# Edge tiles over one fixed range of 16 targets each, and their sums joined by transpositions

## The chip, the cores and the metric

The kernel runs on one core of a Trainium2 chip. The metric is the device time of one execution in microseconds (us), taken as the median of several runs. TensorE (PE) multiplies matrices into PSUM, VectorE (DVE) and ScalarE (ACT) work on rows of up to 128 partitions, GpSimd (POOL) issues gathers by an index list, and SyncE (SP) issues plain transfers. Sixteen DMA engines move the data.

## The reference

A graph layer over 16 batches, 1024 nodes and 256 channels. Only the nonzero entries of `adj` count: there are 9052, about 8.8 for each target v and 19 at most.

```python
pre_u = einsum('bud,dk->buk', h, W1[:d]);  pre_v = einsum('bvd,dk->bvk', h, W1[d:])
hidden = relu(pre_u[:, :, None, :] + pre_v[:, None, :, :] + b1)
S   = sigmoid(einsum('buvk,ko->buvo', hidden, W2)[..., 0] + b2[0])
a_t = einsum('buv,bud->bvd', S * adj, h)
m_t = einsum('uv,bud->bvd', adj, h) * h
z   = beta1 * h + beta2 * (einsum('bvd,de->bve', a_t, Wa) + ba) + beta3 * (einsum('bvd,de->bve', m_t, Wm) + bm)
```

## The kernel before, in words

**Blocks, windows, tiles.** The work goes by 4 groups of 4 batches and 8 blocks of 128 targets: 32 blocks (`order`). A block has 2 windows of 64 targets, and a window 5 tiles of 128 edge slots, so there are 320 tiles. The steps of the main loop (L882) are numbered n by tiles; s is the step within a block (0 to 9).

**Lists.** For each of the 8 blocks of targets `lists` (L242) finds on DVE the sources of each target (up to 24 by `max`), counts them, and gives each target its first slot in its window (`first`, L293 to L310). The 640 slots of a window are 5 tiles of 128. Before the change the window has four quarters of 16 targets: quarter 0 fills from slot 0 upward, quarter 1 from slot 128 on, quarters 2 and 3 fill from their ends downward, so the tiles 0, 1, 3 and 4 are full and the free slots lie in the middle of tile 2. `uidx` holds the source of each slot, and an index beyond the table for an empty one; `val` the entry of `adj`; `onehot` which of 16 targets a slot belongs to. Slot i of a tile lies on partition i.

**One tile.** `fetch` (L515) has POOL issue a gather of up to 128 rows of 8192 bytes from `table[g]`: for the 4 batches of a group the products `pre_u` and the values h of a source. Eight buffers `fetched` take the gathers in turn; a buffer is free again when the sums of its tile are done (`gather_in`, L873), and only then is the gather eight tiles later issued. `expand` (L610, PE) spreads `pre_v` over the slots, `add` (L646, DVE) adds it to the fetched rows, `gate` (L650) takes relu and the product with W2 for 4 batches on DVE (L656), the sigmoid on ACT (L659) and multiplies the one-hot rows by it on ACT (L661). `left_adj` (L619, ACT) has multiplied them by the entry of `adj` (L625).

**Edge sums.** `aggregate` (L664, PE) multiplies the one-hot rows (128 slots by 32 columns: 16 targets, with and without the gate) by the fetched h (128 by 256) for 4 batches, which stand side by side in 4 times 32 columns of PE. That is one pass of 4 multiplications; each shows as two MATMUL in the profile. Before the change a tile holds targets of one or two quarters (`QUARTERS`), so a window takes 1+2+2+2+1 = 8 passes. Two quarters share one PSUM tile `acc` (each its own half); after tile 2 and after tile 4 `half_end` (L678) copies it to `ev` on ACT (L681).

**Turning over.** `turn_over` (L683) transposes `ev` on PE (L691, four transpositions for 32 targets and 256 channels) and copies the result to `LT` on ACT (L694); `times_h` (DVE, L705) multiplies one half by h. It is called twice for a window (q = 0, 1). `block_end` (L710) multiplies `LT` by Wa and Wm (L722), and SP writes the output.

**Other traffic.** SP and ACT also load transposed h for later products, write the tables, and copy h into them (L434, L439, L465); their places are fixed to step numbers. The order on every engine is the order of the code (`manual_schedule`, L492).

## Time and profile before

| What | Value |
|---|---|
| runs of the kernel before | 1075.23 us median; 1073.11 and 1077.70 the others |
| span of the profiled execution | 1080.4 us, 5.2 us above that median |
| busy: PE, DVE, ACT, POOL | 1020.1, 1017.6, 862.6, 459.3 us |
| mean transfer rate | 365 GB/s, 394.56 MB in all |

The profile is of one execution; its groups name a line, an engine, the tiles written and read, the number of instructions, their busy time and mean length, and the idle time ahead of them with what ended it. The view by stages gives for a stretch of the span the busy time of each engine and the mean share of time in which the 16 DMA engines had a packet under way. A share over 1 means that packets of one engine overlap. Beside the views, the trace has a record of each DMA packet: queue, start, length and size.

### The profile page before, as it was taken

What the parts mean: (1) busy time and instruction counts of PE and PEld (TensorE: products, weight loads), DVE (VectorE), ACT (ScalarE), POOL (GpSimd) and SP (SyncE); (2) the same over time, 40 slices, a digit from 0 to 9 for tenths busy, and PEclk for the clock granted to TensorE, in tenths of its full rate; (3) what the DMA queues carried; (4) which work ended last, traced back from release to release, by engine and by line L of the source; (5) the groups of instructions that cost most, each with busy time, mean ns of one, the idle gap of its engine ahead of it and who ended that gap; (6) DMA issues with size and microseconds to landing.
All of it is one profiled execution on the core that took longest, in us unless ns stands there. A gap on an engine that the chain in (4) does not pass through costs nothing.

```text
span 1080.4 us, 24120 instructions
## 1 busy us (share of the span) xinstructions
PE 1020.1 (94%) x7673; PEld 731.3 (68%) x7673; DVE 1017.6 (94%) x3481; ACT 862.6 (80%) x2616; POOL 459.3 (43%) x456
## 2 busy tenths in 40 slices
PE   7777999999999999999999999999999999999996
PEld 6654676776666776677777767777766667666654
DVE  8687999998999999999999999999999999999993
ACT  3246787788888887898888888889889889999983
POOL 2666676555257334553333334333333333333330
PEclk9989999999999999999999999999999999999999
DMA  9999899999999999999999999999999999999991
GB/s 283 327 340 385 313 339 381 362 382 378 403 352 371 408 381 385 379 403 395 404 393 399 412 384 392 408 396 389 381 361 370 369 348 368 365 381 369 365 341 44
DMA packets 147752, 394.56 MB, mean 365 GB/s; under 512 B 18224, under 2 KB 94512, under 8 KB 111408
## 3 DMA queue, kind: packets, MB, share of 16 engines
q0 software_dynamic: 50544, 301.16, 70.9%
q1 hardware_dynamic: 83776, 78.66, 22.9%
q10 hardware_dynamic: 13296, 13.11, 3.5%
q8 instruction: 63, 1.03, 0.4%
q14 instruction: 73, 0.60, 0.1%
HBM read 396.93 MB, written 50.33 MB: 414 GB/s over the span
## 4 chain that ended last, share of the span: by engine, by line
PE 40%; DVE 34%; issue 10%; ACT 8%; DMA 5%; POOL 2%; another core or an unknown queue 0%; POOLq 0%; DVEq 0%; ACTq 0%
DVE fetched L656 16%; DVE fetched L648 12%; PE acc L673 10%; PE misc L722 10%; PE misc L445 9%; PE pc L615 7%; DMA fetched<-table,uidx 3%; PE misc L691 2%; ACT left L661 2%; DVE LT L705 1%; ACT X L489 1%; PE misc L449 1%; DVE low L484 1%; DVE h_blk L737 1%; DMA hT__635<-in_xT_dram 1%
## 5 line engine op out<-in xcount | busy, mean ns | idle before, releaser
L518 POOL DMA_INDIRECT fetched<-table,uidx x320 | 339.4, 1061 | 529.0 <-PE acc L673 389.0
L656 DVE SCALAR_TENSOR_TENSOR fetched<-fetched,w_b 128x256 f32<-128x256 f32 x1280 | 478.0, 419 | 0.0
L648 DVE TENSOR_TENSOR fetched<-fetched,pc 128x1024 f32<-128x1024 f32 x320 | 387.7, 1212 | 29.9 <-PE pc L615 19.4
L661 ACT ACTIVATE left<-left,gt 128x32 f32<-128x32 f32 (+1 forms) x1280 | 299.6, 305 | 10.4
L673 PE MATMUL acc<-fetched,left 128*32 128x256 f32 x4096 | 273.4, 385 | 6.3 <-ACT gt L659 3.7
L615 PE MATMUL pc<-X,mark 128*128 128x512 f32 x640 | 243.7, 462 | 10.9 <-DVE fetched L648 9.3
L673 PEld LDWEIGHTS acc<-fetched,left 128*32 128x32 f32 x4096 | 127.6, 109 | 112.1 <-issue 29.1
L615 PEld LDWEIGHTS pc<-X,mark 128*128 128x128 f32 x640 | 105.4, 189 | 88.9 <-issue 41.6
L659 ACT ACTIVATE gt<-sc,b_b 128x4 f32<-128x4 f32 x320 | 95.9, 300 | 46.7 <-DVE fetched L656 37.5
L722 PE MATMUL misc<-w_m,LT 128*128 128x256 f32 x496 | 117.3, 379 | 0.0
L722 PE MATMUL misc<-w_a,LT 128*128 128x256 f32 x496 | 117.2, 379 | 0.0
L445 PE MATMUL misc<-w_v,hT 128*128 128x256 f32 x448 | 107.6, 383 | 0.0
L722 PEld LDWEIGHTS misc<-w_a,LT 128*128 128x128 f32 x496 | 93.8, 189 | 15.3 <-issue 0.4
L722 PEld LDWEIGHTS misc<-w_m,LT 128*128 128x128 f32 x496 | 93.8, 190 | 15.1
L625 ACT ACTIVATE left<-onehot,val 128x64 f32<-128x64 bf16 (+1 forms) x320 | 102.9, 322 | 0.0
L385 POOL DMA_INDIRECT val<-in_adjT_dram,vidx x80 | 87.2, 1090 | 34.4 <-issue 20.4
L656 DVE DVE_READ_ACCUMULATOR fetched<-fetched,w_b 128x1 f32 x1280 | 100.7, 79 | 0.0
L691 PE MATMUL misc<-ident,ev 128*128 128x128 f32 x512 | 79.5, 278 | 18.5 <-issue 7.0
L445 PEld LDWEIGHTS misc<-w_v,hT 128*128 128x128 f32 x448 | 86.4, 193 | 14.3
L691 PEld LDWEIGHTS misc<-ident,ev 128*128 128x128 f32 x512 | 60.7, 141 | 45.7 <-ACT ev L681 15.2
L482 ACT CAST X<-misc 128x512 fp32r<-128x512 f32 x64 | 37.1, 580 | 55.2 <-PE misc L445 48.0
L445 PE MATMUL misc<-w_u,hT 128*128 128x256 f32 x320 | 76.6, 386 | 4.0 <-issue 3.8
(185 smaller groups left out, 1011.3 us busy)
## 6 DMA issues: line engine op xcount, KB each, us to landing
h_blk<-table SPq DMA_DIRECT2D x62, 256.0 KB
out_dram<-h_blk SPq DMA_DIRECT2D x62, 256.0 KB
hT<-in_xT_dram SPq DMA_DIRECT2D x28, 512.0 KB
table<-in_x_dram ACTq DMA_DIRECT2D x24, 512.0 KB
table<-tab SPq DMA_DIRECT2D x48, 256.0 KB
fetched<-table,uidx POOLq DMA_INDIRECT x320
table<-in_x_dram SPq DMA_DIRECT2D x8, 512.0 KB
table<-fetched SPq DMA_DIRECT2D x8, 512.0 KB
```

Of the source, the lines that this page charges most:

```text
L385: nc.gpsimd.indirect_dma_start(out=val[:, i, j:j + 1], out_offset=None, in_=adj_flat, in_offset=bass.IndirectOffsetOnAxis(ap=vidx[:, i, j: ...
L445: nc.tensor.matmul(p[:, bb * D:(bb + 1) * D], hT[:, 2 * h + bb, i, :], wt[:, i, :], start=(i == 0 and not begun), stop=(i == DC - 1), skip ...
L518: nc.gpsimd.indirect_dma_start(out=fetched[at_slot[n]], out_offset=None, in_=table[g], in_offset=bass.IndirectOffsetOnAxis(ap=uidx[:, vt * ...
L615: nc.tensor.matmul(pcs[n][:, c], marks[n // TW][:, j * P:(j + 1) * P], cuts[k][:, w, c], start=True, stop=True)
L625: nc.scalar.activation(lefts[n][:, :m, 1::GB, :], onehot[:, i, o:o + m, :].unsqueeze(2).to_broadcast([P, m, GB // 2, V]), AF.Copy, scale=v ...
L648: nc.vector.tensor_tensor(t, t, pcs.pop(n), ALU.add)
L656: nc.vector.scalar_tensor_tensor(t[:, b, :], t[:, b, :], 0.0, w2_b, ALU.max, ALU.mult, accum_out=sc[:, b:b + 1])
L659: nc.scalar.activation(gt, sc, AF.Sigmoid, bias=b2_b)
L661: nc.scalar.activation(lefts[n][:, :m, 2 * b, :], lefts[n][:, :m, 1 + b // 2 * GB, :], AF.Copy, scale=gt[:, b:b + 1])
L673: nc.tensor.matmul(accs[h][b * 2 * V:(b + 1) * 2 * V, r, :], left[:, i, 2 * b - b % 2:2 * b - b % 2 + 2].rearrange("p k v -> p (k v)"), f[ ...
L691: nc.tensor.transpose(pt[:, r, :, c, :], ev[:, r, c * P:(c + 1) * P], ident)
L722: nc.tensor.matmul(pz[:, bb * D:(bb + 1) * D], LTs[k][:, 2 * h + bb, i if bb else 1 - i, c, :], wt[:, c, :], start=False, stop=(i == 0 and ...
```

## The change

Each tile of a window now holds targets of one fixed range of 16: the ranges begin at targets 0, 11, 24, 37 and 48 of the window's 64 (`FROM`), so neighbours overlap in 5, 3, 3 and 5 targets. A target's edges go on behind those of the target before it, but the targets from `NEW[j]` on (0, 16, 27, 40, 53) start no earlier than slot 128 j. So every tile fills from its slot 0 upward, and its free slots are its last ones. With these inputs all 9052 edges find a slot in both versions; the windows have 549 to 607 edges, and after the change the emptiest tile holds 84, the fullest 128.

`aggregate` makes one pass for a tile. Two tiles that follow each other share one `acc` (also over a window's or block's end), and `pair_end` copies it to one of four `ev` tiles. `turn_over` turns the five tiles of a window, one half of the channels at each call: five transpositions write into one PSUM tile at their targets' columns, and where ranges overlap, PSUM adds. In the last window (`apart`) each call takes the three tiles that touch its 32 targets, for both halves of the channels. For w = 1 both calls stand at s = 2, one ahead of the step's other work and one behind it (before: s = 0 and s = 2). The lists need one multiplication of 5 columns for `first`, and some DVE instructions less; constants are made by 15 small POOL instructions at the start.

On PE in the middle of the kernel, this is what stands there before the change: one step's sums (L673) of three passes, transpositions of two halves (L691), with the expansion of `pre_v` (L615) between them.

```order
L722 MATMUL misc<-w_m,LT 128x256 x4
L615 MATMUL pc<-X,mark 128x512 x2
L691 MATMUL misc<-ident,ev_10157 128x8x16 x4
L673 MATMUL acc_10231<-fetched_171,left 32x256 x8
L673 MATMUL acc_10231<-fetched_172,left 32x256 x4
L673 MATMUL acc_10305<-fetched_172,left 32x256 x4
L615 MATMUL pc<-X,mark 128x512 x2
L691 MATMUL misc<-ident,ev_10229 128x8x16 x4
L615 MATMUL pc<-X,mark 128x512 x2
L691 MATMUL misc<-ident,ev_10313 128x8x16 x4
```

The corresponding place after the change, where the sums are L632, the transpositions L654, the expansion L580, and the product with Wm L688:

```order
L688 MATMUL misc<-w_m,LT 128x256 x4
L580 MATMUL pc<-X,mark 128x512 x2
L654 MATMUL misc<-ident,ev_9315 128x8x16 x2
L654 MATMUL misc<-ident,ev_9383 128x8x16 x2
L654 MATMUL misc<-ident,ev_9452 128x8x16
L632 MATMUL acc_9506<-fetched_167,left 32x256 x4
L632 MATMUL acc_9506<-fetched_168,left 32x256 x4
L580 MATMUL pc<-X,mark 128x512 x2
L654 MATMUL misc<-ident,ev_9315 128x8x16 x2
L654 MATMUL misc<-ident,ev_9383 128x8x16 x2
L654 MATMUL misc<-ident,ev_9452 128x8x16
L580 MATMUL pc<-X,mark 128x512 x2
```

Two tiles take 8 multiplications in place of 16, and each half of the channels five transpositions, from three `ev`, in place of four for each 32 targets.

On ACT, a window's end before the change: the scaled one-hot rows of the middle tiles have 2 by 16 columns (L661, L625), `ev` is copied twice a window (L681), and `LT` by quarters (L694).

```order
L659 ACTIVATE gt<-sc,b_b 128x4
L661 ACTIVATE left<-left,gt 128x2x16 x4
L625 ACTIVATE left<-onehot,val 128x2x16
L694 COPY LT<-misc 128x2x16x16
L681 COPY ev_11392<-acc_11309 128x512
L659 ACTIVATE gt<-sc,b_b 128x4
L661 ACTIVATE left<-left,gt 128x16 x4
```

And after it (L621 the sigmoid, L623 and L588 the scaled rows, L656 the copy to `LT`, L640 that to `ev`):

```order
L621 ACTIVATE gt<-sc,b_b 128x4
L623 ACTIVATE left<-left,gt 128x16 x4
L588 ACTIVATE left<-onehot,val 128x2x16
L656 COPY LT<-misc 128x8x64 x2
L640 COPY ev_10685<-acc_10670 128x512
L621 ACTIVATE gt<-sc,b_b 128x4
L623 ACTIVATE left<-left,gt 128x16 x4
```

Every tile now has the narrow rows; `ev` is copied every second tile.

The diff, cut to its core:

```diff
--- before.py
+++ after.py
@@ -71,12 +71,12 @@
     E = TW * P
     S = 24
     U = W // 2
-    Q = 4
-    V = W // Q
-    QUARTERS = [[0], [0, 1], [1, 2], [2, 3], [3]]
+    V = 16
+    FROM = [0, 11, 24, 37, 48]
+    NEW = [0] + [v + V for v in FROM[:-1]]
     RC = 5 + S
     BIG = float(N * N)
-    assert D == 256 and DC == 2 and NW == 2 and S % 8 == 0 and TW == Q + 1
+    assert D == 256 and DC == 2 and NW == 2 and S % 8 == 0 and FROM[-1] + V == W and len(FROM) == TW
     const = ctx.enter_context(tc.tile_pool(name="const", bufs=1))
     dram = ctx.enter_context(tc.tile_pool(name="dram", bufs=1, space=bass.MemoryType.DRAM))
@@ -123,59 +123,32 @@
     nc.vector.tensor_scalar(soon, row, float(W), None, ALU.is_lt)
-    MID = TW // 2
     inw = fixed([P, 1], "inw")
     nc.vector.scalar_tensor_tensor(inw, late, -float(W), row, ALU.mult, ALU.add)
...
+    bounds = fixed([P, 2, TW], "bounds")
+    for j in range(TW):
+        nc.gpsimd.memset(bounds[:, 0, j:j + 1], float(NEW[j]))
+        nc.gpsimd.memset(bounds[:, 1, j:j + 1], float(FROM[j]))
+    reached = fixed([P, TW], "reached")
+    nc.vector.tensor_scalar(reached, bounds[:, 0, :], inw, None, ALU.is_le)
+    start_ = fixed([P, TW], "start_")
+    nc.vector.tensor_scalar(start_, upto[:, :TW], float(P), BIG, ALU.mult, ALU.add)
+    nc.vector.tensor_tensor(start_, start_, reached, ALU.mult)
+    nc.vector.tensor_scalar(start_, start_, -BIG, None, ALU.add)
     until = fixed([P, 1], "until")
+    nc.vector.tensor_scalar(bounds[:, 1, :], bounds[:, 1, :], inw, None, ALU.is_le, ALU.add, accum_out=until)
+    nc.vector.tensor_scalar(until, until, float(P), None, ALU.mult)
+    place = fixed([P, TW, V], "place")
+    for j in range(TW):
+        nc.gpsimd.tensor_copy(place[:, j, :], upto[:, FROM[j]:FROM[j] + V])
+    before = fixed([P, P], "before")
+    nc.vector.tensor_scalar(before, upto[:, :P], row, None, ALU.is_gt)
+    nc.vector.tensor_scalar(before[:, W:], before[:, W:], late, None, ALU.mult)
     slot_of = fixed([P, NW, TW], "slot_of")
     for w in range(NW):
         nc.vector.tensor_scalar(slot_of[:, w, :], upto[:, :TW], float(P), row, ALU.mult, ALU.add)
     ident = fixed([P, P], "ident")
     nc.vector.tensor_scalar(ident, upto[:, :P], row, None, ALU.is_equal)
     slot, nth = upto, upto[:, :S]
@@ -195,7 +168,7 @@
     uidx = const.tile([P, NT * NW, TW], I32, name="uidx")
     vidx = const.tile([P, NT * NW, TW], I32, name="vidx")
     val = const.tile([P, NT * NW, TW], FP, name="val")
-    onehot = const.tile([P, NT * NW, 2 * Q, V], mybir.dt.bfloat16, name="onehot")
+    onehot = const.tile([P, NT * NW, TW, V], mybir.dt.bfloat16, name="onehot")
     whose = const.tile([P, NT * NW, E], mybir.dt.uint8, name="whose")
     thr = const.tile([P, NT], FP, name="thr")
     rest = const.tile([P, NT], FP, name="rest")
@@ -283,29 +256,24 @@
         nc.vector.memset(R[:, 3:4], 1.0)
         yield "op"
         nc.vector.tensor_copy(R[:, 4:5], inw)
+        yield "op"
+        ahead_ = lst.tile([P, TW], FP, name="ahead", bufs=4)
+        nc.vector.tensor_scalar(ahead_, reached, R[:, 0:1], None, ALU.mult)
         yield "step"
         pw = aside(vt)
-        for i in range(4):
-            nc.tensor.matmul(pw[:, i:i + 1], sums[:, i].rearrange("p w q v -> p (w q v)"), R[:, 0:1],
-                             start=True, stop=True)
+        nc.tensor.matmul(pw[:, :TW], before, ahead_, start=True, stop=True)
         yield "wait"
         first = R[:, 1:2]
-        from_ = lst.tile([P, 1], FP, name="from", bufs=4)
-        nc.vector.tensor_scalar(from_, pw[:, 1:2], base, low_, ALU.add, ALU.max)
-        yield "op"
-        nc.vector.scalar_tensor_tensor(first, from_, high_, pw[:, 0:1], ALU.min, ALU.add)
-        yield "op"
-        nc.vector.tensor_scalar(from_, pw[:, 2:3], second_, since, ALU.add, ALU.max)
-        yield "op"
-        nc.vector.tensor_tensor(from_, pw[:, 3:4], from_, ALU.max)
+        from_ = lst.tile([P, TW], FP, name="from", bufs=4)
+        nc.vector.tensor_tensor(from_, pw[:, :TW], start_, ALU.add)
+        yield "op"
+        nc.vector.tensor_reduce(first, from_, AX.X, ALU.max)
         yield "op"
         held = lst.tile([P, 1], FP, name="held", bufs=4)
         nc.vector.tensor_scalar(held, first, -1.0, until, ALU.mult, ALU.add)
         yield "op"
         nc.vector.tensor_scalar(held, held, 0.0, R[:, 0:1], ALU.max, ALU.min)
-        yield "op"
-        nc.vector.scalar_tensor_tensor(held, first, from_, held, ALU.is_ge, ALU.mult)
         yield "op"
         nc.vector.tensor_tensor(R[:, 0:1], held, first, ALU.add)
         yield "op"
@@ -369,13 +337,9 @@
         wanted.extend((i, j) for i in range(vt * NW, (vt + 1) * NW) for j in range(TW))
         yield "cut"
         col = L.rearrange("p (w j) r -> p w j r", w=NW)
-        for i in range(2):
-            nc.vector.tensor_tensor(
-                onehot[:, sl].rearrange("p w (q i) v -> p w q i v", i=2)[:, :, :, i, :],
-                place.unsqueeze(1).to_broadcast([P, NW, Q, V]),
-                col[:, :, i:i + Q, 4:5].to_broadcast([P, NW, Q, V]), ALU.is_equal)
-            if i == 0:
-                yield "op"
+        nc.vector.tensor_tensor(
+            onehot[:, sl], place.unsqueeze(1).to_broadcast([P, NW, TW, V]),
+            col[:, :, :, 4:5].to_broadcast([P, NW, TW, V]), ALU.is_equal)
     wanted = []
@@ -619,12 +584,10 @@
     def left_adj(n):
         k, g, vt, w, j = where(n)
         i = vt * NW + w
-        m = len(QUARTERS[j])
-        o = max(2 * j - 1, 0)
-        lefts[n] = wk.tile([P, 2, 2 * GB - 1, V], FP, name="left", bufs=5)
-        nc.scalar.activation(lefts[n][:, :m, 1::GB, :],
-                             onehot[:, i, o:o + m, :].unsqueeze(2).to_broadcast([P, m, GB // 2, V]),
-                             AF.Copy, scale=val[:, i, j:j + 1])
+        lefts[n] = wk.tile([P, 2 * GB - 1, V], FP, name="left", bufs=5)
+        nc.scalar.activation(lefts[n][:, 1::GB, :],
+                             onehot[:, vt * NW + w, j, :].unsqueeze(1).to_broadcast([P, GB // 2, V]),
+                             AF.Copy, scale=val[:, vt * NW + w, j:j + 1])
     running = []
     be1_eye = []
@@ -658,43 +620,47 @@
         gt = wk.tile([P, GB], FP, name="gt")
         nc.scalar.activation(gt, sc, AF.Sigmoid, bias=b2_b)
         for b in range(GB):
-            nc.scalar.activation(lefts[n][:, :m, 2 * b, :], lefts[n][:, :m, 1 + b // 2 * GB, :],
+            nc.scalar.activation(lefts[n][:, 2 * b, :], lefts[n][:, 1 + b // 2 * GB, :],
                                  AF.Copy, scale=gt[:, b:b + 1])
     def aggregate(n):
-        k, g, vt, w, j = where(n)
         left, f = lefts.pop(n), fetched[at_slot[n]]
-        for i, q in enumerate(QUARTERS[j]):
-            h, r = divmod(q, 2)
-            first = j == h * MID and r == 0
-            if first:
-                accs[h] = psa.tile([P, 2, D], FP, name=f"acc{h}")
-            for b in range(GB):
-                nc.tensor.matmul(accs[h][b * 2 * V:(b + 1) * 2 * V, r, :],
-                                 left[:, i, 2 * b - b % 2:2 * b - b % 2 + 2].rearrange("p k v -> p (k v)"), f[:, GD + b * D:GD + (b + 1) * D],
-                                 start=first, stop=(j == q + 1), skip_group_check=True)
-    def half_end(n, q):
-        evs[q] = one.tile([P, 2, D], FP, name=f"ev{q}")
-        nc.scalar.copy(evs[q], accs.pop(q))
+        i, r = divmod(n, 2)
+        if r == 0:
+            accs[i] = psa.tile([P, 2, D], FP, name=f"acc{i % 2}")
+        for b in range(GB):
+            nc.tensor.matmul(accs[i][b * 2 * V:(b + 1) * 2 * V, r, :],
+                             left[:, 2 * b - b % 2:2 * b - b % 2 + 2].rearrange("p k v -> p (k v)"),
+                             f[:, GD + b * D:GD + (b + 1) * D], start=(r == 0), stop=True, skip_group_check=True)
+    def pair_end(i):
+        evs[i] = one.tile([P, 2, D], FP, name=f"ev{i % EVS}")
+        nc.scalar.copy(evs[i], accs.pop(i))
     def turn_over(k, w, q, step):
         if w == 0 and q == 0:
             LTs[k] = one.tile([P, GB, 2, DC, P], FP, name="LT")
         LT = LTs[k]
-        pt = small("pt").rearrange("p (r k c v) -> p r k c v", r=2, c=DC, v=V)
-        ev = evs.pop(q)
-        for i in range(4):
-            r, c = divmod(i, DC)
-            nc.tensor.transpose(pt[:, r, :, c, :], ev[:, r, c * P:(c + 1) * P], ident)
-        v = slice(w * W + q * U, w * W + (q + 1) * U)
-        r = (w * W + q * U) // V
-        nc.scalar.copy(LT.rearrange("p b k c (r v) -> p r (b k c) v", v=V)[:, r:r + 2],
-                       pt.rearrange("p r k c v -> p r (k c) v"))
         apart = k == BS - 1 and w == NW - 1
-        if not apart:
+        n = k * T + w * TW
+        def turn(c, of, v0, v1):
+            pt = small("pt").rearrange("p (k v) -> p k v", v=W)
+            for j in of:
+                i, r = divmod(n + j, 2)
+                nc.tensor.matmul(pt[:, :, FROM[j]:FROM[j] + V], evs[i][:, r, c * P:(c + 1) * P], ident,
+                                 is_transpose=True, start=(j == of[0]), stop=True, skip_group_check=True)
+            nc.scalar.copy(LT[:, :, :, c, w * W + v0:w * W + v1].rearrange("p b k v -> p (b k) v"), pt[:, :, v0:v1])
+        if apart:
+            of = [j for j, v in enumerate(FROM) if v < (q + 1) * U and v + V > q * U]
+            for c in range(DC):
+                turn(c, of, q * U, (q + 1) * U)
+            v = slice(w * W + q * U, w * W + (q + 1) * U)
+        else:
+            turn(q, range(TW), 0, W)
             if not q:
                 return
             v = slice(w * W, (w + 1) * W)
@@ -821,7 +787,9 @@
     def products(n, k, s):
         nonlocal end, parts
         made_rows(n)
-        if (s == 2 and 0 < k < BS) or n == total:
+        if s == 2 and 0 < k < BS:
+            turn_over(k - 1, 1, 0, n)
+        if n == total:
             turn_over(k - 1, 1, 1, n)
         z = 3 if n < ROOM else 4
         if z <= s < z + 4 and 0 < k < BS:
@@ -836,8 +804,8 @@
             turn_over(k, 0, 0, n)
         if s == 7 and k == BS - 1 or s == 8 and n < ROOM:
             turn_over(k, 0, 1, n)
-        if (s == 0 and 0 < k < BS) or n == total - 1:
-            turn_over(k - (s == 0), 1, 0, n)
+        if n == total - 1:
+            turn_over(k, 1, 0, n)
         if n == total - 2:
             end = tail(tails[:2], n)
             next(end)
@@ -875,8 +843,8 @@
         free.append(at_slot.pop(n))
         refill()
         fetch_val(1 + (n % 3 == 0))
-        if (n + 1) % TW in (0, MID + 1):
-            half_end(n, 0 if (n + 1) % TW else 1)
+        if n % 2:
+            pair_end(n // 2)
     done = 0
     for n in range(total + 2):
@@ -904,6 +872,8 @@
         do(n)
         if s == 8 and ROOM <= n < LAST:
             turn_over(k, 0, 0, n)
+        if s == 2 and 0 < k < BS:
+            turn_over(k - 1, 1, 1, n)
         if n >= LAST and n + 2 < total:
             expand(n + 2)
         if n == 1:
```

More of the change, by code (lines that the diff above doesn't have):

```diff
@@ L123 @@
     nc.vector.tensor_scalar(soon, row, float(W), None, ALU.is_lt)
-    MID = TW // 2
     inw = fixed([P, 1], "inw")
     nc.vector.scalar_tensor_tensor(inw, late, -float(W), row, ALU.mult, ALU.add)
-    from_q = fixed([P, NW * Q + 1], "from_q")
-    nc.vector.tensor_scalar(from_q, upto[:, :NW * Q + 1], float(V), row, ALU.mult, ALU.is_le)
-    hv = fixed([P, NW, Q, 1], "hv")
-    nc.vector.tensor_tensor(hv.rearrange("p w q one -> p (w q one)"), from_q[:, :-1], from_q[:, 1:], ALU.subtract)
-    mine = fixed([P, Q], "mine")
@@ L160 @@
-    same = hv.rearrange("p w q one -> p (w q) one").to_broadcast([P, NW * Q, V])
-    nc.vector.memset(sums[:, 1:], 0.0)
-    nc.vector.tensor_scalar(ahead, upto[:, :P].rearrange("p (q v) -> p q v", v=V), row, None, ALU.is_gt)
-    nc.vector.tensor_tensor(ahead, ahead, same, ALU.mult)
-    def of(q, n=1):
-        return hv[:, :, q:q + n, :].to_broadcast([P, NW, n, V])
-    nc.vector.tensor_tensor(sums[:, 0, :, 2:, :], sums[:, 0, :, 2:, :], of(2, 2), ALU.subtract)
-    nc.vector.tensor_copy(sums[:, 1, :, 1:2, :], of(0))
@@ L177 @@
     nc.vector.tensor_scalar(ident, upto[:, :P], row, None, ALU.is_equal)
-    place = upto[:, :W].rearrange("p (q v) -> p q v", v=V)
     slot, nth = upto, upto[:, :S]
@@ L508 @@
     BS = NG * NT
+    EVS = 4
     def where(n):
@@ L650, in gate @@
     def gate(n):
-        m = len(QUARTERS[n % TW])
         t = fetched[at_slot[n]][:, :GD].rearrange("p (b d) -> p b d", b=GB)
```

21 lines of the change are left out of this document (removed).

## The prediction

> **What bounds the kernel now.** I read the page first: busy shares, then the DMA lines.
>
> ```profile
> span 1080.4 us, 24120 instructions
> PE 1020.1 (94%) x7673; PEld 731.3 (68%) x7673; DVE 1017.6 (94%) x3481; ACT 862.6 (80%) x2616; POOL 459.3 (43%) x456
> DMA packets 147752, 394.56 MB, mean 365 GB/s; under 512 B 18224, under 2 KB 94512, under 8 KB 111408
> q0 software_dynamic: 50544, 301.16, 70.9%
> q8 instruction: 63, 1.03, 0.4%
> q14 instruction: 73, 0.60, 0.1%
> ```
>
> PE and DVE are both busy for 94% of the span, so neither alone is plainly the limit, and the gathers (queue q0) take 70.9% of all DMA engine time. Packets of 8 KB and more are 147752 - 111408 = 36344; without those of q8 and q14 (63 + 73) they are 36208, which is 4 groups times the 9052 edges: a row of a gather is one packet, and an empty slot moves none of this size.
>
> Next the view by stages, since shares of the whole span mix different limits.
>
> ```profile
> core 0: us, PE busy (x) PEld busy (x) DVE busy (x) ACT busy (x) POOL busy (x), PEclk, DMA share, GB/s
> 80.00:140.00 60.00, 50.42 (x337) 33.31 (x328) 51.77 (x186) 42.67 (x129) 39.25 (x38) 0.94 0.95 343
> 140.00:200.00 60.00, 56.32 (x438) 40.38 (x437) 58.42 (x216) 45.88 (x139) 38.05 (x39) 1.00 1.01 370
> 200.00:300.00 100.00, 95.94 (x725) 68.89 (x722) 96.92 (x336) 81.18 (x250) 47.93 (x49) 1.00 1.01 378
> 300.00:400.00 100.00, 97.46 (x734) 70.26 (x736) 97.70 (x334) 84.97 (x258) 47.67 (x46) 1.00 1.02 382
> 400.00:500.00 100.00, 96.64 (x730) 69.58 (x723) 98.06 (x330) 82.32 (x252) 49.53 (x48) 1.00 1.03 391
> 500.00:600.00 100.00, 99.70 (x785) 72.13 (x784) 95.75 (x319) 88.38 (x275) 34.84 (x34) 1.00 1.02 399
> 600.00:700.00 100.00, 98.66 (x754) 72.12 (x753) 95.64 (x313) 85.47 (x262) 35.95 (x33) 1.00 1.02 398
> 700.00:800.00 100.00, 99.80 (x775) 72.33 (x774) 96.37 (x315) 87.22 (x268) 34.67 (x33) 1.00 1.01 385
> 800.00:900.00 100.00, 96.47 (x764) 66.94 (x767) 99.28 (x330) 90.62 (x283) 36.48 (x36) 1.00 0.97 365
> 900.00:1000.00 100.00, 98.12 (x778) 70.12 (x771) 100.00 (x334) 90.05 (x279) 36.02 (x36) 1.00 0.97 368
> 1000.00:1050.00 50.00, 47.02 (x387) 31.38 (x386) 50.00 (x173) 43.59 (x139) 17.36 (x17) 1.00 0.98 360
> ```
>
> Three resources stand at the edge at once. From 200 to 800 us the DMA share is 1.01 to 1.03, DVE has 2 to 4% left and PE seems full; from 800 on DVE is full and the DMA share is 0.97. The change cuts PE's work, so the question is what stands next behind PE: DVE, with 910 - 888.1 = 21.9 us of idle time between 140 and 1050 us, and the DMA engines.
>
> Whether the DMA engines are full, and how the gathers lie on them, no view says; the records of single packets do. An 8 KB packet of a gather lasts 309 ns in 76% of cases, at any time of the run, and the next of its engine starts 306 ns after it. By these steps the packets of one engine can be followed. On each engine a gather leaves eight packets: 8 KB ones (R) for filled slots and 4-byte ones (z) for empty slots, then one more of 4 bytes that ends it. From 500 to 1040 us 738 such groups of eight could be read without a break:
>
> ```
> RRRRRRRR 535   RRRRzzzz 46   zzzzRRRR 46   zzzzzzzz 41   all others 70
> ```
>
> So an engine always has the same eight slots of a tile, two runs of four slots that stand next to each other, and what an empty slot leaves free is not given to another engine. Slots dealt out one by one would give groups such as RRzzzzzR; the busiest engine would then go from 568 to 596 filled slots, half of what is summed below.
>
> [...]
>
> **The change part by part.** First the gathers, which the diff does not touch, but whose empty slots it moves. Counted from the lists that the two versions make of these inputs, a window of 640 slots has 566 filled on average, 35.4 for each of the 16 engines' 40. Before, the empty ones are in the middle of tile 2. With runs of four at a distance of 32 or of 64 slots the busiest engine has 586 or 576 of the 640 slots filled that it serves over the 80 tiles of a group (mean 566). After, every tile fills from slot 0 and has at least 84 filled, so by either pairing some engines have all 640: 8 rows of every tile in place of 7.2 to 7.3. The price of a row is the 306 ns step (309 as recorded; 338 ns if all of q0's 70.9% is laid on the 2263 rows of an engine). That is 0.67 rows * 306 ns = 0.21 us a tile (0.8 rows for the other pairing, 0.24 us), over 320 tiles 66 us, where the busiest engine ends last.
>
> Where does it? For each stage, in us on the busiest engine (runs 32 apart, the smaller difference): tiles landed, its rows before and after times 306 ns, packets of everything else (recorded time, a sixteenth), and the sums:
>
> ```
> stage       us tiles  rows before/after  other   sum before  sum after
>   80:140    60   17       124    136      18.2       56.2       59.9
>  140:200    60   15       112    120      24.1       58.4       60.8
>  200:300   100   32       240    256      25.8       99.3      104.2
>  300:400   100   30       219    240      33.1      100.1      106.5
>  400:500   100   31       228    248      32.8      102.6      108.7
>  500:600   100   33       240    264      28.3      101.8      109.1
>  600:700   100   34       248    272      27.2      103.1      110.5
>  700:800   100   33       244    264      21.8       96.4      102.6
>  800:900   100   34       252    272      14.4       91.5       97.6
>  900:1000  100   36       266    288      11.7       93.1       99.9
> 1000:1050   50   18       128    144       7.7       46.8       51.7
> ```
>
> Sums up to 3% over the stage say how far recorded times count overlaps twice. Where the sum after is over both the stage and the sum before, the excess is the loss: 0.8 + 4.2 + 6.4 + 6.1 + 7.3 + 7.3 + 2.6 + 1.7 = 36 us. From 700 on the page's share (1.01, 0.97, 0.97) is 5 to 8 points over the mean engine's sum by steps, because 2% of the packets take over 600 ns, up to 2 us. If half of that is real standing time, the three stages from 700 to 1000 lose about 3, 1.5 and 4 us more; I take 9.
>
> The other terms stand beside this, and their rows are:
>
> ```profile
> L673 PE MATMUL acc<-fetched,left 128*32 128x256 f32 x4096 | 273.4, 385 | 6.3 <-ACT gt L659 3.7 <-ACT left L661 2.4
> L691 PE MATMUL misc<-ident,ev 128*128 128x128 f32 x512 | 79.5, 278 | 18.5 <-issue 7.0 <-ACT ev L681 5.0 <-ACT LT L694 3.2
> L661 ACT ACTIVATE left<-left,gt 128x32 f32<-128x32 f32 x768 | 184.0, 310 | 6.2
> L661 ACT ACTIVATE left<-left,gt 128x16 f32<-128x16 f32 x512 | 115.6, 296 | 4.2
> L681 ACT COPY ev<-acc 128x512 f32<-128x512 f32 x128 | 73.1, 571 | 7.0 <-remote 4.2 <-PE acc L673 2.0 <-PE pc L615 0.5
> L373 DVE TENSOR_TENSOR onehot<-upto,L 128x128 bf16<-128x128 f32 x16 | 4.2, 282 | 0.0
> L298 DVE TENSOR_SCALAR from<-misc,second__104,since 128x1 f32<-128x1 f32 x5 | 1.4, 273 | 0.0
> L266 DVE TENSOR_REDUCE cut<-cand 128x1 f32<-128x8 f32 x8 | 1.3, 156 | 0.0
> POOL fetched L518 <- PE acc L673: 389.0, 119, 5.1
> DVE fetched L648 <- PE pc L615: 19.4, 21, 2.0
> DVE fetched L648 <- DMA fetched<-table,uidx: 2.7, 1, 2.7
> ```
>
> *PE.* Passes fall from 8 to 5 a window: 4096 * 3/8 = 1536 MATMUL less at 273.4/4096 = 67 ns, -103 us busy. Transpositions rise from 512 to 63 * 10 + 12 = 642: 130 * 155 ns = +20 us. PE's 1020 us become some 937. The gain counts only where PE ends last. DVE waited for PE's expansion 19.4 us in all, and with the lighter PE that mostly goes; what is late next there is the gather.
>
> *Earlier release.* POOL waited 389 us for the sums that free a buffer. A tile's sums end some 0.5 us sooner (8 MATMUL less). But from a gather's issue to its first packet the records show 4.5 us in the median: the rows wait in the engines' queues, so an earlier issue lengthens that queue. I take 0; if the queues were empty it would be worth up to 0.5 us a tile.
>
> *ACT.* Gates: 768 * 14 ns = -11 us; copies of `ev`: 160 in place of 128, +18 us; the scaling by `adj` has fewer columns in 192 of 320 tiles. Near 0, on an engine with 10% and more left.
>
> *DVE and the start.* A list loses one of two comparisons (L373, 282 ns), and five small instructions (such as L298, 273 ns) become three (such as L266, 156 ns): 0.4 to 1.1 us for each of eight lists, four of them ahead of the first gather. The constants lose as many. I take -2 us, between 0 and -4. POOL's 15 small instructions go ahead of a memory fill that nobody needs for tens of us: 0.
>
> *Waits.* Both transposition calls of w = 1 now stand in step 2, behind the copy of the last `ev` in step 1. ACT's copy to `LT` behind the second call comes after that step's gate, and PE's next use of that PSUM buffer waits for it: one copy (571 ns, as L681) a block at most, 18 us if PE were the limit, 0 while gathers are. I take 0.
>
> Sum: 36 + 9 - 2 = +43 us. The profiled execution lies 5.2 us above the median; the same +43 on both gives 1075.2 + 43 = 1118 us.
>
> **The rivals.** *PE's relief counts.* If the DMA engines have room after all (their share of 1.0 being packets that wait, not work), PE falls by 83 us and DVE ends: its idle 21.9 us between 140 and 1050 go, 1075 - 22 = 1053 us. For it: DVE waits by name for PE (19.4 us), hardly for a gather (2.7 us). Against it: PE's busy time counts ends that overlap; by the steps from one start to the next (at most 216 ns for 256 columns, 236 for 512, 109 for a transposition) its work fills 90 to 92% of the stages from 500 to 800 us, while the DMA share there is over 1. It decides if an engine's rows can run faster than one in 306 ns. *Empty slots are shared out.* If the DMA engines evened out the rows, bytes and sums would stay as they are, the stages from 200 to 700 could not run faster, and only the start and the last stages gain: 1072 us. The groups speak against it. *Full price everywhere.* If the last three stages have no room, the 0.207 us count for all tiles past 80 us: 303 * 0.207 = 63, 1138 us; DVE at 100% there speaks for both being close. That the lists would leave edges to the slow path behind the main loop is excluded: all 9052 find a slot.
>
> **How the numbers follow.** A measurement of this kernel tells 0.5% from no change, 5.4 us. Busiest engine ends last, as summed: 0.75; full price everywhere: 0.14; PE's relief: 0.07; shared out: 0.04. Low end of the forecast's own case: the lower sums if overlaps are taken out of every packet (3 ns each), which leaves +18 to +27 us, so 1093; upper end the full price, 1138. The range 1092 to 1138 leaves out the two faster cases, 0.11, and a little above. Slower 0.89, same 0.04, faster 0.07.
>
> **What would show it.** After the change the stages between 200 and 700 us should hold 28 to 31 tiles in 100 us in place of 30 to 34, DVE should fall to 88 to 92% there with its wait on L648 named for the gathers, PE's sums to 2560 MATMUL and 171 us, and the mean DMA share below 1.0, since eight engines wait for the other eight. Every group of eight packets should be R's followed by z's, none the other way round. I am wrong if the DMA share stays at 1.02 with more tiles in 100 us, or if DVE is over 98% busy throughout.

## The result, and the profile after

The changed kernel takes 1142.18 us (median of 4 runs, 1136.84 to 1146.02), the kernel before 1076.47 us on the same terms (1073.11 to 1080.33). The ratio is 1.061, with an interval of 1.058 to 1.065: slower, by 66 us. The forecast was 1118 us, with a range of 1092 to 1138, so the direction came true, but the time lies above the range and the size was too small by a third.

The page after, the lines that answer to those of before:

```profile
span 1135.0 us, 21191 instructions
PE 982.7 (87%) x6219; PEld 701.8 (62%) x6219; DVE 1014.5 (89%) x3446; ACT 863.9 (76%) x2650; POOL 467.0 (41%) x471
...
DMA packets 147741, 394.37 MB, mean 347 GB/s; under 512 B 18224, under 2 KB 94512, under 8 KB 111408
...
q0 software_dynamic: 50544, 301.16, 68.1%
```

The bytes of the gathers are those of before (301.16 MB), and PE has less to do, but PE, DVE and the mean DMA engine all have a smaller share of a longer span. No engine on the page is busy all the time. The stages (columns as before):

```profile
200.00:300.00 100.00, 90.59 (x569) 63.22 (x568) 94.17 (x326) 79.18 (x244) 47.13 (x47) 0.95 0.98 362
300.00:400.00 100.00, 82.36 (x503) 59.40 (x502) 83.39 (x273) 71.93 (x223) 43.10 (x43) 0.91 0.95 344
400.00:500.00 100.00, 92.64 (x610) 66.89 (x611) 97.86 (x344) 84.39 (x264) 49.17 (x48) 1.00 0.99 370
500.00:600.00 100.00, 78.20 (x491) 56.41 (x490) 79.70 (x262) 67.65 (x209) 27.55 (x27) 0.92 0.95 358
600.00:700.00 100.00, 94.98 (x607) 68.85 (x606) 92.91 (x303) 86.73 (x273) 34.12 (x32) 0.98 0.94 357
700.00:800.00 100.00, 84.18 (x550) 60.40 (x549) 83.69 (x272) 76.30 (x240) 31.60 (x30) 0.93 0.94 347
800.00:900.00 100.00, 90.65 (x588) 64.41 (x588) 96.66 (x319) 85.43 (x269) 34.00 (x33) 0.98 0.95 366
900.00:1000.00 100.00, 92.84 (x629) 65.45 (x628) 99.47 (x329) 90.90 (x279) 38.28 (x35) 1.00 0.93 353
```

Between 200 and 800 us the DMA share was 1.01 to 1.03 and is now 0.94 to 0.99: in the mean, some of the 16 engines stand idle. The stages from 300, 500 and 700 us are much worse than their neighbours, and there every compute engine has a hole: of DVE's additions (L611), one for each tile, 28, 27 and 29 ran in them, against 31, 33 and 33 before, while the stages from 200 and 400 us hold as many as before (30 and 32) and the one from 600 us one less (32). The groups on the additions, the sums and the transpositions, and the waits for transfers and the like, name the new wait and those holes:

```profile
L611 DVE TENSOR_TENSOR fetched<-fetched,pc 128x1024 f32<-128x1024 f32 x320 | 390.0, 1219 | 41.3 <-DMA fetched<-table,uidx 24.6 <-PE pc L580 12.4 <-issue 1.7
L632 PE MATMUL acc<-fetched,left 128*32 128x256 f32 x2560 | 206.4, 396 | 28.0 <-ACT left L623 27.7
L654 PE MATMUL misc<-ident,ev 128*128 128x128 f32 x642 | 97.1, 282 | 58.5 <-ACT tab L425 38.9 <-ACT low L447 12.9 <-ACT ev L640 3.8
```

```profile
ACT tab L425 <- DMA table<-tab: 37.1, 5, 13.8
DVE fetched L611 <- DMA fetched<-table,uidx: 24.6, 27, 4.0
ACT X L453 <- DMA out_dram<-h_blk: 21.3, 2, 14.8
DVE h_blk L703 <- DMA h_blk<-table: 14.1, 2, 9.8
```

DVE waited 2.7 us for gathers before and waits 24.6 now. The last number of a wait is its longest: ACT stood up to 14 us for a table store, and PE and DVE behind it. On the chain of waits these stores show how long they take:

```profile
494.83 30.60 DMA table<-tab
700.40 33.59 DMA table<-tab
```

How a wait becomes a hole can be followed at one place:

```profile
515.90 1.04 ACT L453 CAST X<-low 64x1024 fp32r<-64x1024 f32 x1 [6.53 <-DMA out_dram<-h_blk]
```

ACT had waited 6.5 us for an output store, and PE 4.4 us behind ACT. From 510.2 to 522.6 us no sums ran on PE and no buffer came free, and POOL issued no gather for 11.2 us, up to 523.7 us. In 2 us some 80 rows of gathers ran before; from 522 to 526 us there were 5 in all.

The groups of eight packets, read as in the prediction (from 500 us on, 532 groups), now all have their filled slots ahead but for 21 of them (the last column: 5 zzzzRRRR and 16 mixed ones). The lists of the changed kernel allow no such group, so these 21 are probably misread:

```
RRRRRRRR 418   RRRRzzzz 61   other R..z 32   rest 21
```

### The profile page after: what moved, and what is told of

It reads as the page before. It is cut to its first block, busy times and chain, and to the rows that moved or that the text cites. A ratio compares the mean times of both kernels' runs of the same rounds, so it can differ in the third digit from the quotient of the medians.

```text
span 1135.0 us, 21191 instructions
## 1 busy us (share of the span) xinstructions
PE 982.7 (87%) x6219; PEld 701.8 (62%) x6219; DVE 1014.5 (89%) x3446; ACT 863.9 (76%) x2650; POOL 467.0 (41%) x471
## 3 DMA queue, kind: packets, MB, share of 16 engines
q0 software_dynamic: 50544, 301.16, 68.1%
## 4 chain that ended last, share of the span: by engine, by line
DMA 32%; DVE 29%; PE 21%; ACT 8%; issue 8%; POOL 1%; ACTq 0%; SPq 0%; POOLq 0%; DVEq 0%
DVE fetched L618 13%; DMA table<-tab 12%; DVE fetched L611 10%; DMA fetched<-table,uidx 10%; PE misc L409 6%; PE misc L688 5%; PE acc L632 4%; DMA out_dram<-h_blk 4%; PE pc L580 3%; DMA hT__2450<-in_xT_dram 2%; ACT left L623 2%; PE misc L654 1%; DMA table<-in_x_dram 1%; POOL fetched L483 1%; ACT LT L656 1%
## 5 line engine op out<-in xcount | busy, mean ns | idle before, releaser
L483 POOL DMA_INDIRECT fetched<-table,uidx x320 | 344.1, 1075 | 576.8 <-PE acc L632 390.9
L611 DVE TENSOR_TENSOR fetched<-fetched,pc 128x1024 f32<-128x1024 f32 x320 | 390.0, 1219 | 41.3 <-DMA fetched<-table,uidx 24.6
L623 ACT ACTIVATE left<-left,gt 128x16 f32<-128x16 f32 x1280 | 288.9, 296 | 10.4
L580 PE MATMUL pc<-X,mark 128*128 128x512 f32 x640 | 247.1, 468 | 41.8 <-DVE fetched L611 21.4
L632 PE MATMUL acc<-fetched,left 128*32 128x256 f32 x2560 | 206.4, 396 | 28.0 <-ACT left L623 27.7
L580 PEld LDWEIGHTS pc<-X,mark 128*128 128x128 f32 x640 | 106.4, 194 | 123.4 <-issue 42.8
L632 PEld LDWEIGHTS acc<-fetched,left 128*32 128x32 f32 x2560 | 80.3, 110 | 118.9 <-ACT left L623 49.0
L621 ACT ACTIVATE gt<-sc,b_b 128x4 f32<-128x4 f32 x320 | 95.7, 299 | 72.0 <-DVE fetched L618 69.0
L654 PE MATMUL misc<-ident,ev 128*128 128x128 f32 x642 | 97.1, 282 | 58.5 <-ACT tab L425 38.9
L654 PEld LDWEIGHTS misc<-ident,ev 128*128 128x128 f32 x642 | 76.8, 144 | 84.1 <-ACT tab L425 46.1
L688 PE MATMUL misc<-w_a,LT 128*128 128x256 f32 x496 | 118.4, 382 | 0.0
L688 PE MATMUL misc<-w_m,LT 128*128 128x256 f32 x496 | 117.3, 379 | 0.0
L618 DVE DVE_READ_ACCUMULATOR fetched<-fetched,w_b 128x1 f32 x1280 | 110.1, 86 | 0.0
L688 PEld LDWEIGHTS misc<-w_a,LT 128*128 128x128 f32 x496 | 94.8, 191 | 15.4 <-ACT LT L656 0.2
L688 PEld LDWEIGHTS misc<-w_m,LT 128*128 128x128 f32 x496 | 93.9, 190 | 14.9
L588 ACT ACTIVATE left<-onehot,val 128x32 f32<-128x32 bf16 x320 | 97.8, 305 | 0.0
L640 ACT COPY ev<-acc 128x512 f32<-128x512 f32 x160 | 91.4, 571 | 3.9 <-PE acc L632 3.4
L453 ACT CAST X<-low 64x1024 fp32r<-64x1024 f32 x64 | 66.8, 1044 | 22.7 <-DMA out_dram<-h_blk 21.3
## 6 DMA issues: line engine op xcount, KB each, us to landing
table<-tab SPq DMA_DIRECT2D x48, 256.0 KB, 17.1
```

The source lines that it names most:

```text
L483: nc.gpsimd.indirect_dma_start(out=fetched[at_slot[n]], out_offset=None, in_=table[g], in_offset=bass.IndirectOffsetOnAxis(ap=uidx[:, vt * ...
L580: nc.tensor.matmul(pcs[n][:, c], marks[n // TW][:, j * P:(j + 1) * P], cuts[k][:, w, c], start=True, stop=True)
L588: nc.scalar.activation(lefts[n][:, 1::GB, :], onehot[:, vt * NW + w, j, :].unsqueeze(1).to_broadcast([P, GB // 2, V]), AF.Copy, scale=val[ ...
L611: nc.vector.tensor_tensor(t, t, pcs.pop(n), ALU.add)
L618: nc.vector.scalar_tensor_tensor(t[:, b, :], t[:, b, :], 0.0, w2_b, ALU.max, ALU.mult, accum_out=sc[:, b:b + 1])
L621: nc.scalar.activation(gt, sc, AF.Sigmoid, bias=b2_b)
```

## The experiments

The theory: the DMA engine with the most rows ends last, and an 8 KB row costs it 306 ns, the commonest step between the starts of two rows before the change. Rows are counted from the lists, with an engine's two runs of four slots 32 slots apart. The rival: the loss comes from the change's own order (transpositions, copies, lighter PE). Times are medians; each ratio is to the kernel before in runs on the same chip, with its interval.

| Kernel | Rows of the busiest engine of 640 | us | Ratio |
|---|---|---|---|
| before | 586 | 1077 | 1 |
| after | 640 | 1142.2 | 1.061 (1.058 to 1.065) |
| e1_after_spread | 596 | 1080.6 | 1.003 (1.001 to 1.006) |
| e2_before_spread | 568 | 1070.7 | 0.994 (0.991 to 0.997) |
| e3_after_tabq | 640 | 1153.4 | 1.070 (1.066 to 1.075) |
| e4_after_pad | 640 | 1142.6 | 1.058 (1.051 to 1.065) |
| e5_before_pad | 640 | 1131.0 | 1.053 (1.046 to 1.060) |
| e6_after_tab3 | 640 | 1136.1 | 1.053 (1.048 to 1.058) |
| e7_after_swap | 580 | 1079.9 | 1.002 (1.000 to 1.005) |
| e8_after_noout | 640 | 1102.2 | 1.023 (1.017 to 1.029) |
| e9_before_halfpad | 615 | 1105.2 | 1.023 (1.020 to 1.027) |
| e10_after_altends | 630 | 1108.0 | 1.032 (1.025 to 1.039) |

**The slots dealt evenly, after.** Column c of a tile stands for another slot number, so that the first 16 k slots of a tile give each engine k rows. Nothing else is changed.

```diff
+    for j in range(TW):
+        for six in range(2):
+            for five in range(2):
+                nc.vector.tensor_scalar(
+                    dealt.rearrange("p (j f m l) -> p j f m l", j=TW, f=4, m=8, l=4)[:, j, 2 * six + five],
+                    ukey[:, :E].rearrange("p (j a l b m) -> p j a b m l", j=TW, a=2, l=4, b=2, m=8)[:, j, five, six],
+                    -1.0, float(N), ALU.mult, ALU.add)
...
-    slot, nth = upto, upto[:, :S]
+    slot, nth = dealt, upto[:, :S]
```

> The changed kernel with its slots dealt over the partitions so that the first 16 k slots of a tile give every DMA engine k rows; all else as changed. The busiest engine then has 596 of its 640 slots filled, the lightest 537 (changed kernel: 640 and 384; before: 586 and 536). Theory of the busiest engine: the loss goes, 1066 to 1090 us. Rival, the change's own order (transpositions at step 2, copies by pairs, lighter PE) costs the time: it stays above 1120 us.

Measured 1080.6 us: 62 of the 66 us are gone by placing the same rows on other partitions. The rival has fallen as the main cause. The dealing evens the rows only if an engine's two runs lie 32 slots apart: with 64, eight engines would still have all 640 by the lists, so the run speaks for 32.

**The same, before.** The edit is the same in the kernel before.

> The kernel before with the same dealing of slots: busiest engine 568 rows, lightest 562, in place of 586 and 536. Theory of the busiest engine: 18 rows of 306 ns less in 80 tiles, 0.07 us a tile, over the 200 tiles in full stages 14 us: 1056 to 1070 us. Rival, the rows of a tile are not what ends: 1073 to 1080 us. (Some one-column scratch tiles of the lists have one buffer in place of four, to make room.)

Measured 1070.7 us, 0.6% faster than before: just above the band, and half of the 14 us. Two of the stages that the 14 us were counted over:

```profile
400.00:500.00 100.00, 99.69 (x772) 72.43 (x764) 98.77 (x338) 85.72 (x264) 51.03 (x50) 1.00 1.03 392
600.00:700.00 100.00, 99.81 (x775) 72.41 (x774) 96.61 (x315) 87.11 (x268) 34.49 (x34) 1.00 1.02 397
```

With the rows even, PE is busy for over 99% there and DVE for 97 to 99%, and the DMA share is still over 1. Which of them took the other half is not shown.

**Table stores on another queue.**

```diff
-                after(step + 1, lambda t=t, c=c: nc.sync.dma_start(table[g][nt * P:(nt + 1) * P, c], t))
+                after(step + 1, lambda t=t, c=c: nc.scalar.dma_start(table[g][nt * P:(nt + 1) * P, c], t))
```

> The changed kernel, its table stores issued from ACT's queue in place of SP's. If the stalls seen on ACT (37 us of waits for table stores, landing after 30 us) are small packets that queue behind other small packets of SP's queue on the full engines, they go: 1105 to 1128 us. If only the rows of the busiest engine count: 1136 to 1147 us, and other waits take their place.

Measured 1153.4 us, worse than the change. ACT hardly waits for the stores by name any more (2.2 us), but for another transfer:

```profile
ACT gt L621 <- DMA hT<-in_xT_dram: 36.9, 3, 13.9
```

That the number is again 37 us is chance. The queue does seem to matter to the stores: those whose landing the trace can follow (nine of 48) land after 7.1 us in the median and 16 at most, in place of 17.1 and 34 (36 of 48).

```profile
table<-tab SPq DMA_DIRECT2D x48, 256.0 KB, 17.1
table<-tab ACTq DMA_DIRECT2D x48, 256.0 KB, 7.1
```

So the wait moved, as the second half of the expectation had it, and 11 us came on top, for which no run shows the reason.

**Every slot filled, after.** Empty slots fetch a real row with weight 0.

```diff
+        nc.vector.tensor_scalar(s_of, k_of, 0.0, row, ALU.is_equal, ALU.mult)
+        nc.vector.tensor_tensor(s_of, s_of, k_of, ALU.add)
-        nc.vector.tensor_scalar(uidx[:, sl].rearrange("p w j -> p (w j)"), k_of, -1.0, float(N), ALU.mult, ALU.add)
+        nc.vector.tensor_scalar(uidx[:, sl].rearrange("p w j -> p (w j)"), s_of, -1.0, float(N), ALU.mult, ALU.add)
```

> The changed kernel with every empty slot fetching a real row (its weight is 0): all 16 engines carry 640 rows over 80 tiles, 13% more bytes in the gathers, the busiest engine as before. Theory of the busiest engine: the time of the changed kernel, 1135 to 1155 us. Rival, bytes or the mean engine count: the gathers' 68.1% of 1135 us grow by 13%, about 1200 us or more.

Measured 1142.6 us, the time of the changed kernel:

```profile
span 1144.0 us, 21206 instructions
...
DMA packets 147741, 433.28 MB, mean 379 GB/s; under 512 B 13472, under 2 KB 89760, under 8 KB 106656
...
q0 software_dynamic: 50544, 340.07, 73.5%
```

39 MB more moved in the same time, at 379 in place of 347 GB/s. So neither the bytes nor the mean rate set the time here; the half of the engines that was less loaded had the room.

**Every slot filled, before.** The same edit in the kernel before, with its eight passes and its order.

> The kernel before, its edge sums in eight passes and its lists as they were, with every empty slot fetching a real row: every engine carries 640 rows over 80 tiles in place of 536 to 586. Theory of the busiest engine: this alone makes the whole loss, 1132 to 1150 us. Rival, part of the loss comes with the change's order of transpositions and copies: 1095 to 1125 us.

Measured 1131.0 us, just under the expected band. Some 53 of the 66 us (1131.0 - 1077.6) arise in a kernel in which nothing but the rows was changed. ACT waits as long for table stores here as in the changed kernel, so these waits come with the rows; in the kernel before they are 0.9 us:

```profile
ACT tab L465 <- DMA table<-tab: 37.4, 8, 7.5
```

The other 12 us are open. The changed kernel waits for output stores and for DVE's loads of h (21.3 and 14.1 us), which this kernel does not, so the rival may hold for them; but the two intervals overlap (1.046 to 1.060 here, 1.058 to 1.065 there), and no run settles it.

**Half of the windows filled, before.** As above, for the first window of each block alone.

> The kernel before with the empty slots of every first window of a block fetching real rows: the busiest engine carries 613 rows over 80 tiles, halfway between 586 (the kernel before) and 640 (all windows filled, 1131 us). Theory of the busiest engine, full price: 27 rows times 4 groups times 306 ns = 33 us, 1105 to 1115 us, at or above the middle. If there were room for some rows first: below 1098 us.

Measured 1105.2 us. By the lists the busiest engine has 615 rows here, two more than the expectation says: 28 us for the first 29 rows, 26 us for the other 25, where 306 ns a row would give 35 and 31 us. There was no free room to use up first.

**Three buffers for the table stores.**

```diff
-            t = big.tile([P, 2 * D], FP, name=f"tab{h}", bufs=1) if tab is None else tab[:, c]
+            t = big.tile([P, 2 * D], FP, name="tab", bufs=3) if tab is None else tab[:, c]
```

> The changed kernel with three buffers for the table halves that are on their way out, in place of one for each half (some small scratch tiles of the lists have one buffer to make room). If the part of the loss that the rows of the busiest engine do not make, some 11 us between tiles 60 and 220, is ACT's waits for these stores (37 us by name): 1125 to 1136 us. If the waits only move to the next transfer: 1137 to 1146 us.

Measured 1136.1 us, between the two bands; the ratio falls from 1.061 to 1.053, and the intervals touch. The store is gone from the waits, and PE now waits for loads of h:

```profile
ACT X L453 <- DMA out_dram<-h_blk: 26.8, 2, 14.1
PEld misc L409 <- DMA hT__2450<-in_xT_dram: 13.9, 1, 13.9
```

A part of the waits is real cost, a part moves. The run does not tell the shares.

**Evener still, after.** In tiles 1 and 3 the halves of the engines are exchanged (`2 * (six ^ j % 2) + five`).

> The changed kernel with slots dealt over the partitions as in the first experiment, and the two halves of the engines exchanged in tiles 1 and 3 of a window: busiest engine 580 rows, lightest 550. If only the rows count, it lies between the kernel before (586 rows) and that kernel with its rows dealt evenly (568): 1070 to 1079 us. If the lighter PE counts once the rows are even: below 1068 us. If the rest of the change costs something: above 1080 us.

Measured 1079.9 us, just above the first band: the lighter PE wins nothing that can be measured, even with the rows as even as before. Nor do the rows: the busiest engine has 16 rows less than in the first experiment, 20 us at 306 ns, and the time is the same (1079.9 and 1080.6 us). So below some 600 rows another limit seems to take over. DVE, busy for 94% of the span here (1013.9 of 1077.9 us), is the likeliest; that is not shown.

**No output stores.**

```diff
-                after(step + 2, lambda hb=hb[h], b=b: nc.sync.dma_start(
-                    out[b:b + 2, vt * P:(vt + 1) * P, :].rearrange("b p d -> p b d"), hb))
```

> The changed kernel without the 62 stores of its output blocks (the output is not written): 992 packets of 1 KB less on each engine, 46 ns each, 46 us. If the busiest engine is full from start to end, all that goes: 1092 to 1104 us. If rows alone are short on it, and small packets fit beside them: 1125 us or more. If waits for these stores (21 us by name) came on top: below 1090 us.

Measured 1102.2 us: 40 of the 46 us of packets that left. That fits packets of any kind counting on the busiest engine, beside its rows. But ACT's waits for these very stores (21.3 us) left with them, and the run does not tell the two apart.

**Tiles from alternate ends, after.**

```diff
+        if j % 2:
+            nc.vector.tensor_scalar(dealt[:, j * P:(j + 1) * P], upto, -1.0, float((j + 1) * P - 1), ALU.mult, ALU.add)
```

> The changed kernel with the slots of tiles 1 and 3 of a window laid from partition 127 down: every tile still has an engine with 8 rows, but no engine has them in all tiles: the busiest has 630 rows over 80 tiles. If an engine's rows over many tiles count: 10 rows times 4 times 306 ns less than the changed kernel, 1124 to 1136 us. If the fullest engine of each single tile counts: 1137 to 1147 us, as the changed kernel.

Measured 1108.0 us, well below both bands: 34 us for 10 rows of the busiest engine. So the fullest engine of each single tile is not what counts: it still has 640 rows in sum. (The first experiment could not tell, since both counts are 596 there.) But the busiest engine's rows over the whole run, times 306 ns, are not all of it either: they give 12 of the 34 us.

## Where the prediction was right, and which step of it failed

**What was right.** The direction and the mechanism: rows stay on the engine of their slot, the change moved the empty slots to one half of the engines, and the other half ends last (1080.6 us when they are dealt out, 1131.0 us when the kernel before is given the same load). PE's relief was hidden, as forecast: its busy time fell from 1020.1 to 982.7 us, and with even rows no time came of it (1079.9 us). That is less than half of what I expected (937 us). The MATMUL count was right (2560), but the sums took 206.4 us in place of 171: the mean busy time of one rose from 67 to 81 ns. PE's longer waits are not the reason, for the first experiment, at 1080.6 us, has 80 ns:

```profile
L644 PE MATMUL acc<-fetched,left 128*32 128x256 f32 x2560 | 203.9, 390 | 27.4 <-ACT left L635 27.0
```

So it comes with the change; that its runs of MATMUL are shorter may be the reason and is not tested. The table of the forecast took an engine's two runs as 32 slots apart, which no trace of the kernel before shows; the first experiment bears it out (1080.6 us by a dealing that evens the rows at 32 and not at 64). The two rivals on the fast side have fallen. Full price everywhere (1138 us) came nearest, by luck: its ground, no room in the last stages, is false, for from tile 220 on the loss is 5.4 us, where 306 ns a row would give 20.

**Which step failed.** The sum let the busiest engine's rows alone make the loss: "36 us" from a table cut by time, waits taken as 0, and the rows' full price, 0.21 us a tile, as the upper end of the range. The runs show waits for other transfers beside the rows: tiles 60 to 220 lost 47.6 us where their rows cost 33.1. To see it, the run is cut by tiles, from one addition of DVE (L648, L611 after) to another, so that before and after hold the same work. Sums are the busiest engine's rows times 306 ns and a sixteenth of all other packets' time, taken from the packet records (runs of slots 32 apart, as above):

```
tiles      before: us    sum      after: us    sum     change
  0:20          74.5    67.9          75.8    71.0       1.3
 20:60         138.7   137.8         144.5   147.1       5.8
 60:220        494.3   501.0         541.9   534.4      47.6
220:319        282.5   259.6         287.9   280.2       5.4
```

*Tiles 20 to 60.* My table had 0.0 and 0.8 us for the stages from 80 to 200 us. It credited a tile to the stage in which its last row landed, and a tile more or less is 4 us in 60: 15 tiles landed there and 17 additions ran. Counted by tiles the busiest engine was as full there (137.8 of 138.7 us) as later.

*Tiles 60 to 220.* These 160 tiles were full before (501.0 to 494.3 us), so the whole price of the rows falls due: 391.7 - 358.6 = 33.1 us. The stages from 200 to 800 us, somewhat more than these tiles, had 34 in my table, so this was seen. 14.5 us more came. The sum after is 98.6% of the time, before 101.4%: the busiest engine now seems to stand still at times, as between 522 and 526 us. The holes are ACT's and DVE's waits for small transfers, some of which land after 30 us (37.1, 21.3 and 14.1 us by name), in which no sum ends, no buffer comes free and no gather is issued. I had looked for waits in the change's own order, not for what a full engine does to the other transfers that cross it. I had also named the wrong wait: DVE was to run at a steady 88 to 92% and to wait for gathers, but between 200 and 700 us it swings from 80 to 98% from stage to stage, and it waits for gathers 24.6 us in all. Of the 14.5 us some 6 come with the rows alone, for e5_before_pad takes 533.4 us for these tiles, 39.1 more than before. That the waits cost something is shown in part (1136.1 us with three buffers); that they make all of the 14.5 us is not.

*From tile 220 on* the loss is 5.4 us; the 1.7 us of the table and the 1.5 and 4 us of the 9 for long packets gave 7. *The start* won more than the 2 us: the first addition ran at 60.1 us in place of 66.3. Part of that is spread between runs, since three other kernels made from the one before had it at 62.3 to 63.5 us. (A small slip beside these: the long packets of the prediction last up to 2.9 us, not 2.)

The two profiled executions differ by 54.6 us, the medians by 65.7: the profiled one after is the fastest of its runs (1136.84 us), that before lies above its median.

**How well the sum holds.** For tiles 60 to 220 of each kernel, time and sum of the busiest engine:

```
kernel               us     sum   sum/us
before             494.3   501.0   1.014
after              541.9   534.4   0.986
e1_after_spread    495.7   509.1   1.027
e2_before_spread   490.1   490.9   1.002
e3_after_tabq      560.6   535.3   0.955
e4_after_pad       547.5   532.3   0.972
e5_before_pad      533.4   530.9   0.995
e6_after_tab3      537.8   540.2   1.004
e7_after_swap      496.5   498.5   1.004
e8_after_noout     517.1   514.3   0.995
e9_before_halfpad  522.9   521.4   0.997
e10_after_altends  519.8   532.6   1.025
```

The sum gives the time of these tiles within 3%, but for the kernel with the moved stores (4.5%). Within these per cents the waits decide, and they leave open why tiles laid from alternate ends are 22 us faster here than the changed kernel at nearly the same sum; no run shows the reason.

**What beats both.** The kernel before with its slots dealt evenly (1070.7 us, ratio 0.994, 0.991 to 0.997) beats both, the one before by 0.6%. Of the change no part has shown a gain to add to it.

## What to carry to other kernels

Where gathers fill the DMA engines, count rows for each engine, not bytes: here 39 MB more on the engines with fewer rows left the time as it was (1142.6 and 1142.2 us), so the slots left empty there had saved nothing, and the same rows on other partitions took 62 us off (1080.6 us). Place empty slots so that every engine has its share over a few tiles, before cutting work elsewhere. When a load on a full resource grows, cut before and after by pieces of work and not by time to see where there is room, and add what the other users of that resource will wait for it (ACT's waits for table stores went from 0.9 to 37.1 us here).

## What the runs showed of the hardware

From one 8 KB row to the next of its engine, 306 ns is the commonest step in the kernels before and after, at 365 as at 347 GB/s in all, and in the kernel before both in the stage from 80 us (343 GB/s) and in that from 500 us (399 GB/s); so the step did not follow the total rate.

Small packets moved slowly beside the gathers. In the changed kernel, between 510 and 516 us SP's queue moved 51 packets of 512 bytes, 73 of 1 KB and 59 of 2 KB beside 265 rows of gathers, 183 packets in 6 us; after the gathers had run dry, between 526 and 528 us, it moved 806 of 512 bytes and 5 of 2 KB beside 39 rows, 811 packets in 2 us. The table store issued at 494.8 us landed 30.6 us later, at 525.4 us, when 5 rows had run in the 4 us from 522 us on.

The granted clock of PE was 0.91 to 0.93 in the stages with the holes (300, 500 and 700 us) and 1.00 in the full ones (400 and 900 us): in these rows it is lower where PE is less busy (78 to 84% against 93%). That it is a consequence and no part of the cause is likely, since e1_after_spread brought the time back with the change's PE work unaltered, at a mean granted clock of 0.982 (0.957 in the changed kernel).
